# Deformable sampling from 8 by 8 patches as 64-row products on the two halves of the array

## The chip, the cores and the metric

The kernel runs on one core of one Trainium2 chip. The metric is the device time of one execution in microseconds (us). The numbers of a single execution come from the hardware profiler: its span runs from the first to the last instruction, and the execution's own device time stands beside it.

## The reference

Two layers follow one another on 32 images of 128 channels and 32 by 32 pixels. Both start with a group norm and end by adding their input. Layer 0 is an encoder to 1024 channels, a long convolution, a gated linear unit (GLU), a layer norm and a decoder. Layer 1 is the part that the change touches: a deformable depthwise convolution of 8 by 8 taps. Cut to what matters:

```python
x = x + layer0(gn(x))                       # encode, convolve, gelu, GLU, layer norm, decode
off = conv3x3_depthwise(gn(x), offset_w) + offset_b        # (B, 2, 64 taps, H, W)
def body(acc, tap):
    off_t, koff_t, w_t = tap
    px = gx[None] + koff_t[0] + off_t[..., 0]
    py = gy[None] + koff_t[1] + off_t[..., 1]
    ix = px * sx - 0.5;  iy = py * sy - 0.5
    # bilinear sample s of gn(x) at (iy, ix), zero outside the image, for all channels
    return acc + s * w_t[None, :, None, None]
acc, _ = lax.scan(body, zeros, (off, koff, wt))
x = x + gelu((acc - bn_mean) * inv + bn_beta)
```

The offsets are shared by all channels; the tap's weight differs by channel. So a sample is a product of an image patch (pixels by channels) with a column of bilinear weights (pixels by output positions), and the tap's weight is applied to the result.

## The kernel before

**Stages.** First comes a small table (`ssm_kernel_table`), then `ssm_convolution` (the encoder and the long convolution, output `y_d` in DRAM), then `main_block`, then a test that sends images whose offsets are larger than `BOUND_X`, `BOUND_Y` through a general routine (`deformable_redo`).

**main_block** interleaves two streams of work in a written-out order. `first_part(b)` is the GLU, layer norm and decoder of image b: 292 matrix products of 128 rows, 128 columns and 512 moving columns, 584 passes, since each fp32 product is a pair of weight load and matmul twice over. `second_part(b)` is the deformable layer of image b. `run_along` takes the next step of the stream that is behind by its planned cost; `measure` is the planned cost of a step of `second_part`. In the steady state the GLU of image b + 2 runs along `second_part(b)`, and the preparation of image b + 1 (`prepare`, a list of steps with due places) hangs on the same steps. So images 0 to 29 are sampled beside a GLU; images 30 and 31 are sampled alone (`ALONE`).

**Preparation.** The nine 3 by 3 taps give the offsets (`taps`, VectorE). `spread` writes them to DRAM in the order (piece, padded column u, tap column j, tap row, y), `gather` reads them back as 128 partitions, and `hat` makes the one-dimensional bilinear weights on ScalarE: 8 positions in x and 16 in y, 24 tables of `HSUB` = 624 values a partition, written to DRAM (`dhat`). `turn` transposes the image and writes it to DRAM as pixels by channels (`vt_d`).

**Sampling.** The padded columns u = x + kx, 1 to 37, are grouped in 17 packs with a common x window of 8 pixels (`PACKS`); a pack has m = 8 to 16 slots (pairs of column and tap column), 254 in an image. A pack is four pieces of two tap rows (`KY2`). For each piece, `load_hat` loads the x weights (`ds`, SBUF tile of 128 partitions by m by 64) and the y weights (`dhy`, the same size), both replicated to the 16 by 8 pixels of a window by the DMA's access pattern, and `weights` multiplies them on VectorE (L1076). Then three products, one for each of the y windows 0, 8 and 16 (`rows_of`), of 128 rows (16 by 8 pixels), 128 channels and m x 2 x ny columns go to a bank of PSUM each (L1119, tile `dps`, four buffers, tag "sam"); VectorE multiplies each with the tap weights into `prod` (L1122, tile `dp`), and GpSimd adds the two tap rows (L1139) and adds the result into the image's accumulator, column by column (L1144, tile `dacc`). The buffers: five of `ds`, four of `dhy`, three of `prod`.

**Queues.** All loads of hats, windows and `y_d` are issued in the written order by SyncE (queue q1); writes of hats and outputs by ScalarE (q10); the convolution's output `y_d` by GpSimd (q0). Each engine runs its instructions in the written order.

## Time and profile before

| what | value |
|---|---|
| median of 3 runs | 13423.51 us (13420.09 to 13425.37) |
| profiled execution, its own device time | 13421.61 us |
| its span | 13419.9 us, 133500 instructions |
| mean granted TensorE clock | 0.988 |
| TensorE matmul busy | 12998.3 us, 97% of the span |
| VectorE busy | 8388.1 us, 63% |
| ScalarE busy | 3279.7 us, 24% |
| GpSimd busy | 9064.3 us, 68% |
| SyncE's DMA queue (q1) | 2591.60 MB, 72.0% of 16 engines' span |

How to read it: matmuls (PE) and weight loads (PEld) are shown as two rows of one engine, and since matmuls are pipelined, the mean duration of one is longer than the distance between two starts. The distance of starts is what a pass costs in a stream. "x" counts passes, two for each fp32 product. A stage is read in its own window: the convolution takes until 1280 us; then come two GLU images alone; then 30 images of sampling beside a GLU; and from 12880 us two images of sampling alone.

### The profile page before, as it was taken

What the parts mean: (1) busy time and instruction counts of PE and PEld (TensorE: products, weight loads), DVE (VectorE), ACT (ScalarE), POOL (GpSimd) and SP (SyncE); (2) the same over time, 40 slices, a digit from 0 to 9 for tenths busy, and PEclk for the clock granted to TensorE, in tenths of its full rate; (3) what the DMA queues carried; (4) which work ended last, traced back from release to release, by engine and by line L of the source; (5) the groups of instructions that cost most, each with busy time, mean ns of one, the idle gap of its engine ahead of it and who ended that gap; (6) DMA issues with size and microseconds to landing.
All of it is one profiled execution on the core that took longest, in us unless ns stands there. A gap on an engine that the chain in (4) does not pass through costs nothing.

```text
span 13419.9 us, 133500 instructions
## 1 busy us (share of the span) xinstructions
PE 12998.3 (97%) x40482; PEld 7208.8 (54%) x40482; DVE 8388.1 (63%) x12173; ACT 3279.7 (24%) x4767; POOL 9064.3 (68%) x8871
## 2 busy tenths in 40 slices
PE   7998999999999999999999999999999999999975
PEld 7998445555555555555555555555555555555533
DVE  5554146666666666666666666666666666666677
ACT  4433122222222212112222222211122222221245
POOL 2554147777777777777677777777777777777778
PEclk8999999999999999999999999999999999999988
DMA  7998068888888888888888888888888888888866
GB/s 232 274 284 267 19 172 235 240 235 236 232 230 240 236 228 228 233 231 239 237 237 232 229 239 239 231 225 232 231 240 236 236 232 231 236 240 232 232 194 174
DMA packets 1721768, 3055.43 MB, mean 228 GB/s; under 512 B 445523, under 2 KB 1024467, under 8 KB 1720019
## 3 DMA queue, kind: packets, MB, share of 16 engines
q1 hardware_dynamic: 1508434, 2591.60, 72.0%
q10 hardware_dynamic: 163456, 320.92, 6.6%
q0 software_dynamic: 49152, 134.28, 3.3%
q8 instruction: 328, 5.37, 0.2%
q14 instruction: 398, 3.25, 0.1%
HBM read 2580.03 MB, written 466.06 MB: 227 GB/s over the span
## 4 chain that ended last, share of the span: by engine, by line
PE 86%; DMA 7%; DVE 2%; ACT 2%; issue 1%; POOL 1%; SPq 1%; ACTq 0%; DVEq 0%; POOLq 0%
PE gpg L785 24%; PE gpv L808 24%; PE dps L1119 23%; PE psy L320 5%; DMA ds<-dhat 4%; PE gph L824 3%; PE gpo L713 3%; PE psz L237 3%; DMA dhat<-dh 1%; DVE ds L1076 1%; DMA dhy<-dhat 1%; ACT ds L1068 1%; SPq L1057 0%; DMA u<-u_d 0%; DVE dp L1122 0%
## 5 line engine op out<-in xcount | busy, mean ns | idle before, releaser
L1122 DVE TENSOR_TENSOR dp<-dps,k_weight_slots 128x256 f32<-128x256 f32 (+17 forms) x6528 | 3085.4, 483 | 3084.2 <-PE dps L1119 2908.7
L1119 PE MATMUL dps<-ds,dxw 128*128 128x256 f32 (+18 forms) x13056 | 4698.9, 447 | 227.5 <-DVE ds L1076 185.6
L1144 POOL TENSOR_TENSOR dacc<-dacc,dp 128x256 f32<-128x256 f32 (+3 forms) x4736 | 4403.9, 930 | 398.3 <-DVE dp L1139 28.5
L1119 PEld LDWEIGHTS dps<-ds,dxw 128*128 128x128 f32 x13056 | 2468.8, 192 | 3213.9 <-issue 2543.1
L785 PE MATMUL gpg<-gy,g_w_glu 128*128 128x512 f32 x8192 | 3986.4, 593 | 22.9 <-DMA gy<-y_d 18.2
L808 PE MATMUL gpv<-gy,g_w_glu 128*128 128x512 f32 x8192 | 3974.7, 592 | 0.0
L1139 POOL TENSOR_TENSOR dp<-dp 128x448 f32<-128x448 f32 (+2 forms) x2142 | 2671.9, 1247 | 1898.1 <-DVE dp L1122 1895.4
L1076 DVE TENSOR_TENSOR ds<-ds,dhy 128x1024 f32<-128x1024 f32 (+3 forms) x2176 | 3163.4, 1454 | 783.3 <-DMA ds<-dhat 675.5
L785 PEld LDWEIGHTS gpg<-gy,g_w_glu 128*128 128x128 f32 x8192 | 1544.5, 190 | 1237.0 <-issue 968.4
L808 PEld LDWEIGHTS gpv<-gy,g_w_glu 128*128 128x128 f32 x8192 | 1548.9, 189 | 1157.9 <-issue 915.1
L846 POOL TENSOR_TENSOR gs<-gs,gq 128x512 f32<-128x512 f32 x448 | 633.0, 1413 | 1348.2 <-ACT gq L845 1348.2
L845 ACT ACTIVATE gq<-gr 128x512 f32<-128x512 f32 x448 | 282.2, 630 | 4665.5 <-DVE gr L837 4603.9
L357 POOL DMA_DIRECT2D y_d<-yo x1024 | 589.5, 583 | 694.1 <-ACT yo L344 624.6
L792 ACT ACTIVATE gs<-gpg,k_b_glu 128x512 f32<-128x512 f32 x512 | 351.8, 687 | 2494.1 <-PE gpg L785 2378.0
L981 ACT ACTIVATE dh<-dr,k_minus 128x624 f32<-128x624 f32 x768 | 621.7, 809 | 654.7 <-DMA dhat<-dh 574.2
L320 PE MATMUL psy<-toe,z 128*128 128x192 f32 x4096 | 668.0, 326 | 7.4 <-DVE z L242 5.5
L320 PEld LDWEIGHTS psy<-toe,z 128*128 128x128 f32 x4096 | 663.0, 196 | 11.6 <-DVE z L242 6.8
L816 DVE SCALAR_TENSOR_TENSOR gs<-gpv,k_b_glu,gs 128x512 f32<-128x512 f32 x512 | 379.9, 742 | 437.2 <-PE gpv L808 436.8
L982 ACT ACTIVATE dh<-dh,one 128x624 f32<-128x624 f32 x768 | 626.2, 815 | 25.0
L715 POOL TENSOR_TENSOR gs<-gs,gr 128x512 f32<-128x512 f32 x448 | 631.7, 1410 | 0.0
L824 PE MATMUL gph<-gu,k_W_enc 128*128 128x512 f32 x1024 | 525.9, 595 | 30.1 <-DVE gs L816 30.1
L335 DVE TENSOR_TENSOR psy<-psy,t 128x256 f32<-128x256 f32 (+2 forms) x768 | 333.7, 434 | 346.1 <-ACT t L328 329.3
(163 smaller groups left out, 5810.3 us busy)
## 6 DMA issues: line engine op xcount, KB each, us to landing
dhy<-dhat SPq DMA_DIRECT2D x1536, 512.0 KB
ds<-dhat SPq DMA_DIRECT2D x1440, 512.0 KB
dhat<-dh ACTq DMA_DIRECT2D x768, 312.0 KB
y_d<-yo POOLq DMA_DIRECT2D x1024, 128.0 KB, 4.2
gy<-y_d SPq DMA_DIRECT2D x512, 256.0 KB
u<-u_d SPq DMA_DIRECT2D x224, 512.0 KB
dxw<-dvt_d SPq DMA_DIRECT2D x1248, 64.0 KB
dhy<-dhat SPq DMA_DIRECT2D x256, 224.0 KB
```

The costliest lines, as they stand in the source:

```text
L320: nc.tensor.matmul(ps[:, c // 2, c % 2, :], rows[i][:, (g * CG + c0 + c) // 2, c % 2, :], toe[:, c0 + c, :], start=True, stop=True,)
L715: nc.gpsimd.tensor_add(sums[0], sums[0], r)
L785: nc.tensor.matmul(gate, w_glu[:, k, D + m * P : D + m * P + P], ys[k], start=(k == 0), stop=(k == KD - 1),)
L808: nc.tensor.matmul(val, w_glu[:, k, m * P : m * P + P], ys[k], start=(k == 0), stop=(k == KD - 1),)
L824: nc.tensor.matmul(h, w_enc[:, m * P : (m + 1) * P], u, start=True, stop=True)
L846: nc.gpsimd.tensor_add(sums[1], sums[1], sq)
L982: nc.scalar.activation(t, t, AF.Relu, scale=-1.0, bias=const["one"])
L1076: nc.vector.tensor_mul(s[:, :m], s[:, :m], hy[:, :m])
L1119: nc.tensor.matmul(ps, xw[:, j, :], s[:, :m, :, y0 : y0 + ny], start=True, stop=True)
L1122: nc.vector.tensor_mul(prod[:, :m, :, y0 : y0 + ny], ps, w[:, :, :, None].to_broadcast([P, m, KY2, ny]),)
L1139: adder.tensor_add(prod[:, :m, 0], prod[:, :m, 0], prod[:, :m, 1])
L1144: nc.gpsimd.tensor_add(to, to, prod[:, slot : slot + nj, 0])
```

## The change

A sample now comes from a patch of 8 by 8 pixels. Such a product has 64 rows, and two of them lie on the two halves of the array: "side" 0 on partitions 0 to 63 and side 1 on 64 to 127, each with its own weights (`xw[half, w]`), moving columns and PSUM bank. The padded rows v = y + ky, 1 to 37, are dealt to the sides: 1 to 19 to side 0 and 19 to 37 to side 1 (`NV`, `VBASE`); each side has seven y windows of 8 rows at steps of 2 (`NWIN`). The hats are stored in DRAM as (side, position, u, j, ky, 19 rows), 8 positions in x and 8 in y; a tile of them (`ds`, `dhy`) holds one column u, or two in the packs with four columns (`groups_of`), as 128 partitions by up to 9 slots by 152 cells.

A pack is four pieces again (`blocks_of`): piece 0 holds the ends in five small blocks of 2 to 4 rows, and pieces 1 to 3 hold four values of v for all eight tap rows, in two windows each. For each block, window, hat tile and side there is one product. Two pieces make a burst: all products of pieces 0 and 1 are issued together, into four PSUM banks, then the products of the other stream go on, then come the VectorE products with the tap weights (`scale`), one (piece, side) to a step, then the `weights` of a tile of the next pack, in two parts. At the end of a pack GpSimd adds the eight tap rows, which stand in `prod` as rows of 512 values, shifted so that equal y lie under each other, by seven additions, and then adds the total into the accumulator. `prod` is two fixed tiles, cleared once. The buffers: four of `ds` and two of `dhy`, four temporaries for the GLU in place of five; the software descriptor scratch is set to 4096 bytes.

In the preparation, offsets go to DRAM in two steps: `lay` writes them as they are with gaps (`rel_n`), and `spread` copies them from there, DRAM to DRAM, in runs of 19 values, four times an image; `window` copies the image's windows from `vt_d` to `xw_d`, DRAM to DRAM, 16 times an image; there are 16 hat tables of `HSUB` = 741 values in place of 24 of 624. `BOUND_Y` falls from 3.25 to 2.45. The special handling of images 30 and 31 (a loaded quarter of the x weights that ScalarE copies, and one VectorE addition) is gone.

The diff's core:

```diff
+NV = 19
+VBASE = (1, 19)
+CELLS = 8 * NV
+PIECES = 4
+SIDE = NU * 8 * CELLS
+NCOL = 2 * SIDE
...
-BOUND_X, BOUND_Y = 2.45, 3.25
+NWIN = 7
+BOUND_X, BOUND_Y = 2.45, 2.45
...
+def groups_of(us):
+    if len(us) < 3:
+        return tuple((u,) for u in us)
+    return us[:2], us[2:]
+
+def blocks_of(side, piece):
+    if piece == 0:
+        ends = (
+            (0, 2, 1, 6, 1, 0), (2, 2, 3, 4, 1, 0), (4, 2, 5, 2, 1, 0), (2, 3, 2, 1, 2, 2)
+        ) if side == 0 else (
+            (6, 2, 32, 6, 1, 0), (4, 2, 32, 4, 1, 0), (2, 2, 32, 2, 1, 0), (1, 3, 32, 1, 2, 2)
+        )
+        w = 6 * side
+        return [(b, [(w, 0, b[3])]) for b in ends] + [
+            ((4 * side, 4, 19, 1, 1, 0), [(6 - w, 0, 1)])
+        ]
+    v0 = (7, 20)[side] + 4 * (piece - 1)
+    w = 2 * (piece - 1) + side
+    return [((0, 8, v0, 4, 1, 0), [(w, 0, 2), (w + 1, 2, 4)])]
...
-    SB, HB = 5, 4
+    SB, HB = 4, 2
...
+            def lay(a):
+                    nc.sync.dma_start(at(rel_n[b % 2], a * ASTEP + LEAST + 7 * JSTEP,
+                            [[KSTEP, 8], [-JSTEP, 8], [1, L]]), ...)
+            def spread(a, side):
+                    nc.sync.dma_start(
+                        at(rel_d[b % 2], a * NCOL + side * SIDE,
+                            [[NV, 64], [8 * CELLS, NU], [1, NV]]),
+                        at(rel_n[b % 2], a * ASTEP + LEAST - 7 * H + VBASE[side],
+                            [[KSTEP - 1, 64], [H, NU], [1, NV]]))
...
+            def window(side, r):
+                    nc.sync.dma_start(st["xw_d"][side, :, r],
+                        at(st["vt_d"], (12 * side + r) * W * C,
+                            [[C, W], [2 * W * C, NWIN], [1, C]]))
...
             steps = [
...
-                (71, largest), (74, across), (79, down), (81, spread(0)), (82, spread(1)),
-                (89, gather(0)), (90, gather(1)),
-                *((96 + 82 * i // len(hats), step) for i, step in enumerate(hats)),
+                *((54 + i, window(i // 8, i % 8)) for i in range(16)),
+                (68, largest), (70, across), (74, down), (76, lay(0)), (77, lay(1)),
+                *((81 + 3 * i, spread(i // 2, i % 2)) for i in range(4)),
+                (99, gather(0)), (100, gather(1)),
+                *((106 + 72 * i // len(hats), step) for i, step in enumerate(hats)),
...
+        def weights(h, part):
+            m = sum(span_of(u)[1] for u in halves[h][1])
+            cut = slice(0, (m + 1) // 2) if part == 0 else slice((m + 1) // 2, m)
+            nc.vector.tensor_mul(s_of[h][:, cut], s_of[h][:, cut], hy_of[h][:, cut])
+            if part == 1:
+                hy_of.pop(h)
+                load_hat(h + HB, 1)
...
+                for i in range(0, PIECES, 2):
...
+                    for piece in (i, i + 1):
+                        ps = [psam.tile([P, 512], F32, tag="sam", ...) for side in range(2)]
+                        for parts in zip(blocks_of(0, piece), blocks_of(1, piece)):
+                            for part in range(len(parts[0][1])):
+                                for s, count in zip(tiles_s, counts):
+                                    for side in range(2):
+                                        half = slice(64 * side, 64 * side + 64)
...
+                                        nc.tensor.matmul(
+                                            to[side][:, slot : slot + count, :, r0:r1],
+                                            xw[half, w, :], frm, start=True, stop=True)
+                    yield measure(m)
...
+                    for j in range(4):
+                        due(1 + j)
+                        scale(i + j // 2, j % 2)
+                        yield measure(m)
+                    due(5)
+                    if i // 2 < len(ahead):
+                        weights(ahead[i // 2], 0)
+                        yield measure(m) / 2
+                        weights(ahead[i // 2], 1)
+                    yield measure(m) / 2
+                for h in mine:
+                    load_hat(h + SB, 0)
+                for to, frm in ((2, 0), (3, 1), (4, 6), (5, 7), (2, 4), (3, 5), (2, 3)):
+                    nc.gpsimd.tensor_add(row(to), row(to), row(frm))
...
-    nc = _bacc.Bacc("TRN2", target_bir_lowering=False, num_devices=1)
+    nc = _bacc.Bacc("TRN2", target_bir_lowering=False, num_devices=1, dynamic_dma_scratch_size=4096)
```

## The prediction

> **What bounds the kernel now.** I read the page first: engines, slices, the chain of waits.
>
> ```profile
> PE 12998.3 (97%) x40482; PEld 7208.8 (54%) x40482; DVE 8388.1 (63%) x12173; ACT 3279.7 (24%) x4767; POOL 9064.3 (68%) x8871
> PEclk8999999999999999999999999999999999999988
> DMA  7998068888888888888888888888888888888866
> PE gpg L785 24%; PE gpv L808 24%; PE dps L1119 23%; PE psy L320 5%; DMA ds<-dhat 4%; PE gph L824 3%; PE gpo L713 3%; PE psz L237 3%; DMA dhat<-dh 1%; DVE ds L1076 1%; DMA dhy<-dhat 1%; ACT ds L1068 1%; SPq L1057 0%; DMA u<-u_d 0%; DVE dp L1122 0%
> ```
>
> TensorE sets the time, at full clock. Then the windows: nine images of the steady state, and the two images sampled alone.
>
> ```profile
> core 0: us, PE busy (x) PEld busy (x) DVE busy (x) ACT busy (x) POOL busy (x), PEclk, DMA share, GB/s
> 5368.00:8681.00 3313.00, 3294.60 (x9039) 1691.43 (x9039) 2147.76 (x3017) 692.78 (x918) 2391.35 (x2214) 1.00 0.86 234
> 12880.00:13164.00 284.00, 172.54 (x420) 91.36 (x420) 216.93 (x310) 181.13 (x195) 214.27 (x202) 0.79 0.65 189
> 13164.00:13420.00 256.00, 149.00 (x404) 79.89 (x404) 199.22 (x295) 134.12 (x135) 215.14 (x202) 0.85 0.61 175
> ```
>
> An image costs 3313 / 9 = 368.1 us; in it TensorE is idle for 2 us, VectorE busy for 239, GpSimd for 266, the DMA engines for 86%. Only the last two images wait for something else. Third, the groups of those nine images:
>
> ```profile
> L1119 PE MATMUL dps<-ds,dxw 128*128 128x256 f32 (+17 forms) x3674 | 1314.3, 440 | 10.6 <-DVE dp L1122 10.5
> L785 PE MATMUL gpg<-gy,g_w_glu 128*128 128x512 f32 x2304 | 1128.3, 593 | 1.0 <-DVE gs L816 1.0
> L1076 DVE TENSOR_TENSOR ds<-ds,dhy 128x1024 f32<-128x1024 f32 (+3 forms) x612 | 890.1, 1454 | 213.6 <-DMA ds<-dhat 203.8 <-DMA dhy<-dhat 5.7 <-DMA dhat<-dh 3.8
> L1122 DVE TENSOR_TENSOR dp<-dps,k_weight_slots 128x256 f32<-128x256 f32 (+13 forms) x1837 | 870.3, 483 | 906.2 <-PE dps L1119 859.3 <-POOL dacc L1144 29.6 <-POOL dp L1139 7.1
> L1139 POOL TENSOR_TENSOR dp<-dp 128x512 f32<-128x512 f32 (+3 forms) x612 | 762.4, 1246 | 549.8 <-DVE dp L1122 549.0
> L1144 POOL TENSOR_TENSOR dacc<-dacc,dp 128x256 f32<-128x256 f32 (+6 forms) x1332 | 1237.4, 929 | 104.5
> ```
>
> Sampling is 3674 / 9 = 408 passes an image. Last, what a pass costs in a stream, from the chain in order of time (start, us, what): one GLU pass of 512 columns is 1.72 / 4 = 0.43 us, one pass of 128 columns 41.50 / 368 = 0.113 us.
>
> ```profile
> 284.70 41.50 PE psz L237 x368
> 4999.64 1.72 PE gpv L808 x4
> ```
>
> So the GLU's 584 passes take 251 us of the 368 (eight transposes 1 more), and sampling holds TensorE for 116 us an image, 6.8 us a pack. This is what the change must beat.
>
> **TensorE after.** Products of a pack: piece 0 has 5 blocks x 2 hat tiles x 2 sides = 20, pieces 1 to 3 have 2 windows x 2 tiles x 2 sides = 8 each, 44 in all (22 in the pack of one column), 16 x 44 + 22 = 726 an image, 1452 passes with 128 moving columns or fewer (16 to 96 in piece 0, 128 or less in the others). The moving columns of a side are 127 a slot where the full array had 256. But fewer columns do not make a pass cheaper here, since each has a weight load of its own. The trace shows loads as the limit where matmuls are short (sixteen products of one column, at clock 0.50):
>
> ```profile
> L653 PEld LDWEIGHTS g_fold<-k_ln_beta,k_W_dec x16: 286/333/333, 1297.0 to 1300.1; 128*128 128x128 f32 x16
> 1296.00:1304.00 8.00, 6.71 (x31) 6.66 (x32) 1.81 (x9) 0.00 (x0) 0.00 (x0) 0.50 0.63 164
> ```
>
> Fifteen steps in 3.1 us are 0.21 us a load at half clock, 0.105 at full clock: as much as a pass of 128 columns. So a pass is 0.112 us, long or short, and everything hangs on how the two sides overlap, which no row shows: every product before has 128 rows. Bounds: full overlap 1452 x 0.112 / 2 = 81 us an image; none, 163 us. I take 81, since the sides share neither rows, weights, columns nor bank, and keep 163 for the range.
>
> The Trainium skill's "TensorE: Matmul & The Clock Gate" (Part 3: Packing small matmuls) says that matmuls on different row groups run together, with 3.07 times the rate measured for four groups at 512 columns; no run here shows it. By that rate, 1.53 for two groups, the products would take 163 / 1.53 = 106 us and the total be 13540; its case has long matmuls, behind which loads hide.
>
> Entering and leaving the 64-row form: 34 bursts, 68 changes an image. No row prices one. Nothing, if the array takes both forms side by side; at most one matmul's tail and a load: a 128-column pass lasts at least 276 ns where starts are 112 apart, so 0.164, plus a load's 0.19, makes 0.35 us. That is 0 to 24 us an image; I take the tail alone, 11 us, as loads are seen to run under matmuls in flight. The page "TensorEngine Tiling (Array Packing)" (Tiling Modes, Key Properties) speaks against the change: changing the tiling mode drains the array. No run here shows it; by that rule a change costs at least the tail, 11 us an image, and without it nothing.
>
> **VectorE.** From L1122's forms (256 values 415 ns, 480 values 655) an operation is 141 ns + 1.07 a value. Per full pack, 10 small ones of piece 0 (48 to 192 values) and 6 of 512 make 6.6 us, 107 an image (now 97). `weights` goes from 68 operations of mostly 1024 values (512 values 839 ns, 1024 1528: 150 + 1.35 a value) to 66 of mostly 608, some 0.94 us each: 62 us in place of 890.1 / 9 = 99. Sum: 239 + 10 - 37 = 212 us, beside TensorE. But it is coupled more tightly: a burst takes all four banks, so it waits for the previous burst's four scalings, and the first burst of a pack for the weights issued 0.5 step before it. Between bursts TensorE has half a pack of GLU, 7.4 us; VectorE then has 2.8 to 3.9 us of scaling, 2 of weights, about 0.7 of GLU. Where nine `taps` (1.32 us each) or a layer norm's closing (some 7 us) join, it lags by 2 to 3 us a few times an image: 6 us an image in place of 2, range 2 to 20. Behind a waiting burst stand the GLU products, so this goes straight to the end.
>
> **GpSimd.** 68 additions of two tap rows (1.25 us) become 17 x 7 of about 1.2 (144 us), the 148 into `dacc` become 37 (34 us): 178 against 222. Off the path; two `prod` tiles give a pack of slack.
>
> **DMA.** Hats fall from 66.6 MB an image (254 x 256 x 4 B x 128 x 2) to 39.5. New: 4 x 2496 runs of 76 bytes and 3584 of 512, DRAM to DRAM. 128-byte packets take 15 ns of an engine in the trace, 512-byte ones 32: 9 and 7 us of the 16 engines together, far under what the hats free (27 MB, some 110 us of transfer). All go through SyncE's queue, ahead of hat loads; a `window` there also waits for `vt_d` to land. I cost this at nothing: it is covered by tiles loaded a pack ahead, and if that cover fails a stall like today's 10 us at `ds<-dhat` comes a few times an image. The smaller descriptor scratch touches only the convolution's stores: GpSimd waits 42 us for those in all now; nothing. The reference's inputs give offsets of at most 2.38 in x and 2.10 in y, under 2.45, so no image goes to the general routine.
>
> **Sum.** An image: 251 + 1 + 81 + 11 + 6 = 350 us against 368, 18 less; 30 images, 540. The two images alone take 284 and 256 us; their chain runs over loads, VectorE and ScalarE's copy, which is gone. VectorE then needs 169 us, GpSimd 178, products 92: with the coupling I take 230 each, 80 us less in all (0 to 140). From the profiled execution's 13421.6 us (span 13419.9): 13421.6 - 620 = 12800. The median of the runs is 2 us higher, which is nothing beside the rest. A difference of 0.2% (27 us) is about what can be told from no change. This case alone, with 0 to 24 us of changes and 2 to 20 of waits: 12450 to 13300.
>
> **The rivals.**
> *The loads go one at a time* (slower). Place: the weight load in each of 1452 passes. In the trace a load starts when the matmul before it starts, and in the written order both passes of side 0 precede those of side 1, so side 1 may never start early. Price: 163 us in place of 81, an image of 432, 30 x 64 = 1920 more, tail 60 less: 15280. It decides from the point where a pass costs over 0.068 us: (116 - 17) / 1452. For it: the fold's even load spacing, and every stream above. Against: those are loads into the same rows.
> *Half overlap.* Side 1's first pass runs beside side 0's second, but each side's own second load waits: some 0.288 us a pair (two loads 0.21, plus two starts of 34 to 40 ns after a load, the fold's 68 at half clock). 363 x 0.288 = 105 us, image 374, + 180 - 80: 13500, 13250 to 13750.
> *The bound moves to VectorE or the hat loads.* VectorE needs 212 of 350 us and is not it on average; a lag at each burst of 3 us (34 x 3 = 102 us) would undo everything: 30 x (344 + 102 - 368) - 80 more, some 15700. Little speaks for it but the coupling.
>
> **How the numbers follow.** Full overlap 0.47, half 0.21, loads one at a time 0.26, VectorE or transfers 0.06. Faster: nearly all of the first and a quarter of the second, 0.50; same 0.04; slower 0.46. The range must take in part of the loads' case to leave out 0.2: 12450 to 15300.
>
> **What would show it.** Right: 1452 passes an image at `dps`, starts of the two sides within some tens of ns, a burst of pieces 2 and 3 in about 1.8 us; images 350 us apart; PE still busy over 95% in the steady state; DMA share near 0.7; VectorE near 212 us an image. Wrong: passes evenly 0.11 us apart and bursts of 3.6 and 6.3 us (loads), image distance over 368; or idle PE before bursts released by `dp` or `ds` (VectorE). A gap over 0.35 us at the edges of bursts would fail the price of a change.

## The result

The changed kernel takes 14571.98 us, the median of four runs (14553.06 to 14581.83), and the kernel before 13424.44 beside it: a ratio of 1.0851, interval 1.0832 to 1.087. It is 1148 us slower where 624 faster was forecast. The profiled execution has a span of 14577.5 us.

First the page of the changed kernel: busy time, TensorE's clock and the DMA share in 40 slices, and the chain of waits by line.

```profile
PE 13374.9 (92%) x73890; PEld 8152.3 (56%) x73890; DVE 7794.9 (53%) x14251; ACT 2697.3 (19%) x3983; POOL 7930.1 (54%) x6987
...
PEclk9999999999999999999999999999999999999955
DMA  7986277777777777777777777777777777777776
...
PE gpv L837 16%; PE dps L1208 15%; DMA ds<-dhat 14%; PE gpg L814 13%; DVE ds L1132 8%; PE psy L320 5%; DVE prod L1225 3%; PE psz L237 3%; DMA dxw<-dxw_d 3%; PE gpo L742 2%; DMA dhy<-dhat 1%; PE gph L853 1%; SPq L1120 1%; SPq L734 1%; DMA dh
```

TensorE is no longer what sets the time throughout. Its share falls from 97% to 92%, and "DMA ds<-dhat", the x-hat loads, rises from 4% of the chain to 14%, as much as TensorE's products or either half of the GLU. The DMA engines are busy for 70 to 79% in most slices. Then the windows, in the columns of before: eight steady images and the two sampled alone.

```profile
core 0: us, PE busy (x) PEld busy (x) DVE busy (x) ACT busy (x) POOL busy (x), PEclk, DMA share, GB/s
5454.40:8662.80 3208.40, 3017.18 (x16390) 1712.69 (x16386) 1765.09 (x3210) 537.15 (x689) 1834.61 (x1490) 0.94 0.75 159
13872.00:14244.00 372.00, 195.47 (x1558) 178.80 (x1558) 193.82 (x377) 41.48 (x48) 190.84 (x159) 0.56 0.73 156
14244.00:14577.00 333.00, 170.30 (x1365) 158.45 (x1364) 158.25 (x327) 2.30 (x2) 185.16 (x159) 0.57 0.67 129
```

An image costs 3208.40 / 8 = 401 us. TensorE is idle for 24 of them, ten times as long as before, and the clock is 0.94. The DMA engines were busy for 86% at 234 GB/s before; now for 75% at 159, so an engine's busy time brings a fifth less. The two images alone run at little more than half the clock. The groups of those images show each term of the prediction's sum:

```profile
L1254 POOL TENSOR_TENSOR prod<-prod 128x512 f32<-128x512 f32 (+3 forms) x952 | 1265.3, 1358 | 673.4 <-DVE prod L1225 662.8
...
L1208 PE MATMUL dps<-ds,dxw 64*128 64x128 f32 (+6 forms) x11622 | 894.4, 307 | 144.2 <-DVE ds L1132 90.1 <-DMA dxw<-dxw_d 52.2 <-DVE prod L1225 0.4
...
L1225 DVE TENSOR_TENSOR prod<-dps,k_weight_slots 128x512 f32<-128x512 f32 (+14 forms) x2176 | 781.8, 407 | 594.1 <-PE dps L1208 408.6 <-POOL prod L1254 132.0 <-DVE prod L1225 2.3
L1132 DVE TENSOR_TENSOR ds<-ds,dhy 128x608 f32<-128x608 f32 (+2 forms) x530 | 593.5, 1158 | 585.9 <-DMA ds<-dhat 542.2 <-DMA dhy<-dhat 20.2 <-DMA dxw<-dxw_d 12.0
...
L1260 POOL TENSOR_TENSOR dacc<-dacc,prod 128x256 f32<-128x256 f32 (+6 forms) x296 | 198.6, 671 | 23.2
```

VectorE's products now wait for "DMA ds<-dhat" for 542.2 / 8 = 68 us an image, against 203.8 / 9 = 23 before. The engine is not short of time (1765 / 8 = 221 us busy). Its tiles are late.

To separate work from waiting, images are cut where the memset of `dacc` starts, over 20 steady images. Idle time of TensorE and the work that half clock loses (half of the busy time in the stretches with a granted clock of 0.5) are taken off, and what is left is TensorE's work at full clock. In us an image:

| kernel | image | idle | lost to half clock | work | the two images alone |
|---|---|---|---|---|---|
| before | 368.2 | 2.2 | 0.2 | 365.8 | 533 |
| after | 400.5 | 23.4 | 20.3 | 356.8 | 697 |
| e1: y-hats in one load, 16 engines | 387.8 | 16.2 | 14.2 | 357.4 | 575 |
| e2: the same rows in two loads, 8 engines | 397.4 | 22.3 | 18.1 | 357.0 | 678 |
| e3: y-hats issued by GpSimd | 382.3 | 15.7 | 8.9 | 357.7 | 580 |
| e4: before, y-hats in two loads | 437.9 | 51.4 | 15.3 | 371.2 | 654 |
| e5: no copies | 380.5 | 10.5 | 13.4 | 356.7 | 677 |
| e6: e3, spread by GpSimd too | 379.2 | 13.9 | 8.0 | 357.3 | 592 |
| e9: e3 and e5 | 364.5 | 3.8 | 3.1 | 357.6 | 561 |
| e13: e3, spread in 16 parts | 372.2 | 7.8 | 6.9 | 357.5 | 572 |
| e15: e3, no spread | 364.0 | 3.7 | 2.6 | 357.6 | 559 |
| e17: e3, spread in 32 parts | 364.0 | 3.3 | 3.3 | 357.4 | 587 |

The change did make TensorE's work 9 us an image shorter; but idle time and half clock together rose from 2 to 44 us.

### The profile page after: what moved, and what is told of

It reads as the page before. It is cut to its first block, busy times and chain, and to the rows that moved or that the text cites. A ratio compares the mean times of both kernels' runs of the same rounds, so it can differ in the third digit from the quotient of the medians.

```text
span 14577.5 us, 194927 instructions
## 1 busy us (share of the span) xinstructions
PE 13374.9 (92%) x73890; PEld 8152.3 (56%) x73890; DVE 7794.9 (53%) x14251; ACT 2697.3 (19%) x3983; POOL 7930.1 (54%) x6987
## 4 chain that ended last, share of the span: by engine, by line
PE 55%; DMA 22%; DVE 14%; issue 4%; SPq 3%; ACT 1%; POOL 0%; DVEq 0%; ACTq 0%; POOLq 0%
PE gpv L837 16%; PE dps L1208 15%; DMA ds<-dhat 14%; PE gpg L814 13%; DVE ds L1132 8%; PE psy L320 5%; DVE prod L1225 3%; PE psz L237 3%; DMA dxw<-dxw_d 3%; PE gpo L742 2%; DMA dhy<-dhat 1%; PE gph L853 1%; SPq L1120 1%; SPq L734 1%; DMA dhat<-dh 1%
## 5 line engine op out<-in xcount | busy, mean ns | idle before, releaser
L1254 POOL TENSOR_TENSOR prod<-prod 128x512 f32<-128x512 f32 (+3 forms) x3808 | 5057.7, 1357 | 2900.9 <-DVE prod L1225 2858.2
L1208 PE MATMUL dps<-ds,dxw 64*128 64x128 f32 (+14 forms) x46464 | 3700.6, 313 | 842.8 <-DVE ds L1132 384.9
L1225 DVE TENSOR_TENSOR prod<-dps,k_weight_slots 128x512 f32<-128x512 f32 (+16 forms) x8704 | 3128.0, 407 | 2345.8 <-PE dps L1208 1641.5
L1208 PEld LDWEIGHTS dps<-ds,dxw 64*128 64x128 f32 x46464 | 3371.4, 212 | 1722.5 <-issue 959.9
L814 PE MATMUL gpg<-gy,g_w_glu 128*128 128x512 f32 x8192 | 3915.1, 622 | 199.9 <-DMA gy<-y_d 196.7
L837 PE MATMUL gpv<-gy,g_w_glu 128*128 128x512 f32 x8192 | 3832.5, 611 | 0.0
L1132 DVE TENSOR_TENSOR ds<-ds,dhy 128x608 f32<-128x608 f32 (+2 forms) x2112 | 2371.3, 1161 | 2384.4 <-DMA ds<-dhat 2174.6
L1260 POOL TENSOR_TENSOR dacc<-dacc,prod 128x256 f32<-128x256 f32 (+6 forms) x1184 | 797.0, 673 | 92.9
L1022 ACT ACTIVATE dh<-dr,k_minus 128x741 f32<-128x741 f32 x512 | 464.3, 907 | 1143.1 <-DMA dr<-rel_d 776.8
L237 PE MATMUL psz<-w_enc,u 128*128 128x128 f32 x4096 | 495.7, 284 | 18.2 <-issue 10.5
```

The costliest lines, as they stand in the source:

```text
L237: nc.tensor.matmul(both[:, g, j, :], u[:, lo : lo + P], w_enc[:, k * P : (k + 1) * P], start=True, stop=True,)
L814: nc.tensor.matmul(gate, w_glu[:, k, D + m * P : D + m * P + P], ys[k], start=(k == 0), stop=(k == KD - 1),)
L837: nc.tensor.matmul(val, w_glu[:, k, m * P : m * P + P], ys[k], start=(k == 0), stop=(k == KD - 1),)
L1132: nc.vector.tensor_mul(s_of[h][:, cut], s_of[h][:, cut], hy_of[h][:, cut])
L1208: nc.tensor.matmul(to[side][:, slot : slot + count, :, r0:r1], xw[half, w, :], frm, start=True, stop=True,)
L1225: nc.vector.tensor_mul(bass.AP(tensor=at_y.tensor, offset=at_y.offset, ap=[at_y.ap[0], [H, m], [step * (KS - 1) + skew, rows], [1, run],], ...
```

## The experiments

Times are medians; e2, e4, e5, e8, e9 and e15 are one execution each. Two theories stood against each other and against a third. A: the y-hat loads (tile `dhy`) of 64 partitions run on 8 of the 16 DMA engines, so that the x-hats (tile `ds`) that share these engines come late. B: the copies from DRAM to DRAM (`lay`, `spread`, `window`) hold the loads up. The rival C is the prediction's own last one: VectorE, or tiles asked for too late, so that what remains late is late for lack of buffers.

**e1 and e2: sixteen engines or eight.** In the trace of the changed kernel just 8 DMA engines are at work for 19.6% of the steady time (before 1.6%); which ones, the trace does not say. A y-hat load reads with an outermost dimension of 8. e1 makes it one load with 16 outermost, by which the y-hats of a side come in another order and the sums are wrong; e2 keeps this order of rows but two loads:

```
-   for side in range(2): ... at(src, frm + side * 8 * SIDE, [[0, 8], [SIDE, 8], [1, nj * CELLS]])
+e1 at(src, frm, [[SIDE, 16], [0, 8], [1, nj * CELLS]])                              # one load
+e2 for side in range(2): ... at(src, frm + side * 8 * SIDE, [[SIDE, 8], [0, 8], [1, nj * CELLS]])
```

> The changed kernel with each tile of y weights (dhy) loaded by one transfer whose outermost dimension has 16 entries, in place of two whose outermost dimension has 8. The 16 source rows and the bytes are the same, but within a side the rows are laid out in the order of the x weights, so the samples use wrong y weights; all else is as in the change. Theory T1 (the eight-row transfers run on only 8 of the 16 DMA engines, which are then full): no more stretches with exactly 8 active packets (now 20% of the time), VectorE's wait for ds<-dhat falls from 68 us an image to under 15, images 360 to 370 us apart in place of 401, total 13200 to 13450. Rival R1 (the DRAM-to-DRAM copies in SyncE's queue delay the hats) and rival R2 (too few tiles, loads issued too late): image distance stays within 2% of 401, total 14300 to 14600. Rival R3 (the 64-row products or their change of form hold TensorE): total as the change, 14570.

> As the run above it (same source rows and same wrong order of y weights), but again two transfers of 64 partitions whose outermost dimension has 8 entries. It tells the number of engines apart from the order of the rows. T1: as the change, images 395 to 405 us apart, total 14500 to 14700. If the row order were what matters: as the run above.

Measured: e1 14089.93 us, ratio to before 1.0496 (1.0478 to 1.0513); e2 14481.19. The stretches with exactly 8 engines at work fall to 1.2% in e1 and stay at 16.2% in e2. So one load over 16 engines in place of two over 8 is worth 391 us, the order of the rows at most 91. The size of the whole effect was missed: e1 is 664 us over the time before.

**e3: the same loads from another queue.** The two y-hat loads are left as they are, issued by GpSimd.

```
-   nc.sync.dma_start(to[side * 64 : side * 64 + 64], ...)
+   nc.gpsimd.dma_start(to[side * 64 : side * 64 + 64], ...)
```

> The changed kernel with the y weights' transfers issued by GpSimd in place of SyncE, otherwise the same transfers and the same result. T1 if that queue's eight engines rotate from transfer to transfer: no more stretches at exactly 8 active packets, images 365 to 380 us apart, total 13300 to 13800 (74 issues of about 0.6 us more an image on GpSimd, which is at half load). T1 if they are the same eight: as the change, 14500 to 14800. R1: a gain of at most half, since the copies then delay only ds: 14000 to 14500. R2 and R3: as the change.

Measured: 13926.23 us, ratio 1.0366 (1.0349 to 1.0383), 646 us less than the changed kernel. Exactly 8 engines: 3.6% of the time. The wait of VectorE for x-hats falls from 542 to 113 us in a window of eight images. A holds, with an image 18 us shorter, and 15.7 us of idle TensorE remain; the total is 126 us above the range that A had.

**e4: the cut alone, in the kernel before.** Its y-hat load is split into two of 64 partitions; nothing else is touched.

```
-   dims = [[[0, rows], [NCOL, 8]], [[NCOL, rows], [0, 8]]][a]     # one load, 16 outermost
+   for top in range(2): ... at(..., [[NCOL, 8], [0, 8], [1, m * SLOT]])
```

> The kernel before with each load of y weights cut into two transfers of 64 partitions whose outermost dimension has 8 entries; same bytes, same result, 68 issues more an image. T1: the low eight engines must carry 33.3/8 + 33.3/16 MB of hats and 1.1 MB of the rest an image, 7.4 MB, which at 16 GB/s an engine (4096 bytes in 254 ns) takes 460 us: images over 440 us apart, total over 15600. R1, R2, R3: within 1% of 13424, since the copies, the buffers and the products are those of before.

Measured: 15638.62 us, 2212 more than before, with images 437.9 us apart (over 440 was expected) and exactly 8 engines at work for 23.3% of the steady time. From its page, clock, DMA share, rate and the group of `weights`:

```profile
PEclk9999999999999999999999999999999999999987
DMA  7893377777777777777777777777777777777753
GB/s 236 277 283 118 114 195 194 193 202 196 197 196 193 198 203 202 191 203 197 194 193 195 194 200 186 196 207 201 193 196 193 198 196 199 194 195 203 191 169 134
...
L1086 DVE TENSOR_TENSOR ds<-ds,dhy 128x1024 f32<-128x1024 f32 (+3 forms) x2176 | 2834.8, 1303 | 5456.7 <-DMA ds<-dhat 4354.0
```

"ds<-dhat" becomes the longest wait of `weights`, as in the changed kernel, although the x-hat loads were not touched. This shows A by itself, but for one rival: the cut also makes more loads, and each issue takes SyncE some 0.6 us. The traces speak against it. SyncE's issues of loads take 154 us in an image of 368 before, 138 of 400 after the change and 216 of 438 in e4, and for most of the rest it waits. That the cut costs more here than in the changed kernel fits the hats, of which before loads 1.7 times the bytes.

**e5: no copies.** `lay`, `spread` and `window` return at once from the third image on.

> The changed kernel with the DRAM-to-DRAM copies (the image into lay, spread, and window) left out from the third image on, so that later images sample with the places and windows of the first two; everything else is as it was. In the changed kernel's trace TensorE's idle time in eight steady images is 24 us an image, and 14 of it lies in a few places at the eighth and ninth of the 17 packs, just where the four spread copies are issued; SyncE's issues of spread and of the loads behind it take up to 13.6 us there, where before none took over 2.3. Theory (SyncE's queue stands behind spread): the idle time at those packs goes, with some slow clock after it, and images come 13 to 22 us closer, 14570 to some 13870 - 14150, and the issues take 0.3 to 2.5 us. Rival (only the y-hat loads on 8 engines matter): no more than the copies' own DMA time, some 16 us of 16 engines an image of which little is on the path: 14400 to 14570. Rival (no copies on the path, VectorE's coupling is the rest): 14500 to 14570.

Measured: 13996.39 us, 20 us an image less, as B's theory had it. The idle time at the ninth pack, the one of one column, is gone (12.2 us an image from its first product to the next pack's in the changed kernel, 0.0 now); the waits for "ds<-dhat" that A explains are still there, 374 us in 2900.

**e9: both.** e3's and e5's edits together.

> The y-hat loads issued by GpSimd (e3) and the copies lay, spread and window left out from the third image on (e5), both in one kernel. In the changed kernel a steady image of 400.5 us is 356.8 of TensorE's work at full clock, 23.4 of idle TensorE and 20.3 lost to half clock; e3 alone took 18.2 us off an image, e5 alone 20.0, neither changed the 357. Theory (these two are the whole stall): together they take off 36 to 42, an image is 359 to 364 us with under 3 us of idle, and the total 13230 - 13400 with e3's shorter tail. Rival (a third cause, such as VectorE's lag behind the bursts, takes over): an image of 368 to 380, 13550 to 13850.

Measured: 13392.19 us, within the theory's range; an image is 364.5 us, 3.8 of it idle, each a little above what the theory had. Apart, the two edits took 18.2 and 20.0 us off an image; together 36.0. So A and B are all but some 7 us of the stall, and VectorE's coupling (C) has at most these. The two also lie in different places: e3 takes the idle time of the other packs from 11.2 us an image to 3.4 and leaves 12.3 at the ninth, e5 clears the ninth and leaves 10.5 at the others.

**e6, e7, e10: is it the queue, or the number of buffers?** e3's timeline of SyncE's queue, at an eighth pack (start, us, what):

```profile
8127.48 24.14 SPq L990 DMA_DIRECT2D rel_d<-rel_n  x3
8151.72 4.81 SPq L734 DMA_DIRECT2D gy<-y_d  x3
8156.62 6.04 SPq L1115 DMA_DIRECT2D ds<-dhat  x2
8162.71 2.01 SPq L1146 DMA_DIRECT2D dxw<-dxw_d  x2
8164.82 1.08 SPq L734 DMA_DIRECT2D gy<-y_d  x2
...
8172.84 0.54 SPq L1115 DMA_DIRECT2D ds<-dhat  x1
8176.27 2.13 SPq L1146 DMA_DIRECT2D dxw<-dxw_d  x2
```

Three issues of `spread` hold SyncE's queue for 24 us, and inputs of the GLU, x-hats and windows stand behind them. In the same kernel's view of transfers, over 8130 to 8165 us, the DMA engines are at least 80% busy in nine slices in which they bring less than 100 GB/s (slices of 0.9 us, busy tenths and rate):

```profile
DMA  6899899999999998669589989757336999899798
GB/s 117 273 306 263 260 299 220 229 211 255 168 183 186 118 76 36 58 78 97 34 139 247 168 58 25 13 18 49 23 21 41 62 80 61 66 124 115 110 165 207
```

e6 issues `spread` from GpSimd; e7 adds an x-hat tile, e10 a third window tile loaded two packs ahead, both with hat tiles of 8 columns in place of 9 (e7 also with 10 GLU tiles in place of 11).

```
e6  -   nc.sync.dma_start(at(rel_d[b % 2], ...      +   nc.gpsimd.dma_start(at(rel_d[b % 2], ...
e7  -   SB, HB = 4, 2                               +   SB, HB = 5, 2
e10 -   windows(b, n + 1)                           +   windows(b, n + 2)
```

> The changed kernel with the y-hat loads and the four spread copies issued by GpSimd in place of SyncE: the same transfers. With the y-hat loads alone moved (e3) it was 13926 and an image 382.5 us, 15.8 us of it idle TensorE, nearly all of that at the eighth and ninth packs. Theory (SyncE's queue stands behind spread): that idle time and the slow clock after it go, an image comes to 364 - 372 us and the total to 13350 - 13650. Rival (spread's 2496 small pieces load the DMA engines or hold GpSimd's queue as they held SyncE's, so the y-hat loads are late in place of the others): 13800 to 14100.

> As e6, with one more x-hat tile (5 in place of 4), so that the tile needed first in a pack is asked for a pack earlier; room for it comes from tiles of 8 columns in place of 9 (the packs of four columns are paired otherwise) and from 10 GLU input tiles in place of 11. Theory (what remains late in e6 is x-hats): 0 to 10 us an image less than e6, and no wait of VectorE for x-hats. Rival (what remains is the passes' own price and slow clock after the bursts): within 40 us of e6, or slower by up to 100 if the GLU's inputs come late with 10 tiles.

> As e6 (y-hat loads and spread issued by GpSimd), with three window tiles, loaded two packs ahead in place of one; room for the third comes from hat tiles of 8 columns in place of 9, with the packs of four columns paired otherwise. In e6 12.9 of 13.9 us of idle TensorE an image lie at the eighth and ninth packs, and the longest waits there are for the window tile (84.5 us in 2900, longest 11.2): the ninth pack has one column and is half as long, so a load asked for at its start has half the time. Theory (windows late behind the spread pieces): that idle time goes, an image is 364 to 370, the total 13400 to 13600. Rival (the spread pieces make whatever is loaded then late, and y-hats or x-hats wait in its place): 13750 to 13870.

Measured: e6 13861.01 us (ratio 1.0325, 1.0308 to 1.0343), e7 13876.11 (1.033, 1.0306 to 1.0353), e10 13840.89 (1.031, 1.0292 to 1.0327). All three theories fell, and the totals are in the rivals' ranges. In e6 no issue on SyncE takes over 4.6 us while images are sampled, but the idle time stays at the same packs: now the window tile and y-hats are late. First e6 (us in total over 2900, times, longest):

```profile
PE dps L1208 <- DMA dxw<-dxw_d: 84.5, 16, 11.2
DVE ds L1132 <- DMA dhy<-dhat: 74.0, 8, 12.2
```

In e10 the window tile is in time, and y-hats and x-hats are late:

```profile
DVE ds L1132 <- DMA dhy<-dhat: 59.0, 10, 11.8
DVE ds L1132 <- DMA ds<-dhat: 46.6, 10, 13.1
```

In e7 the wait for x-hats is gone, as its theory had it, and y-hats are late for 84 us; its rival's reason, the passes' own price, is not what remains. So it is not SyncE's queue alone and not the number of buffers: what is loaded beside `spread` lands late, from either queue.

**e11, e13, e17: the same copies at other times.** e11 issues the four copies in the ninth and tenth packs. e13 cuts them into 16 parts, 2.5 steps apart; e17 into 32, 1.5 steps apart over four packs, and has the three unread matmuls of e16 (below) besides.

```
e11 +   *((106 + 3 * i, spread(i // 2, i % 2)) for i in range(4)),
e13 +   *((79 + 5 * i // 2, spread(i // 8, i // 4 % 2, i % 4)) for i in range(16)),   # [[NV, 16], [8 * CELLS, NU], [1, NV]]
e17 +   *((79 + 3 * i // 2, spread(i // 16, i // 8 % 2, i // 2 % 4, i % 2)) for i in range(32)),   # half of NU each
```

> As e6, with the four spread copies issued at steps 106 to 115 (the ninth and tenth packs) in place of 81 to 90, and gather and the hats after them moved to 124 to 175. Theory (the spread pieces meet the half-long one-column pack by their place): the idle time falls by half or more, an image is 366 to 373, the total 13450 to 13650. Rival (wherever they are issued, some 14 us of idle and slow clock follow): 13800 to 13900. Should the hats come too late for the next image, over 13900.

> y-hat loads issued by GpSimd (as e3), all copies kept on SyncE's queue, but spread cut into 16 parts of 624 pieces, issued 2.5 steps apart (79 to 116, some 5 us between two) in place of four of 2496 at 81 to 90; gather and hats follow at 102 and 121, and 108 to 173. In e3 four such copies keep the 16 engines 88% busy for some 20 us at 84 GB/s. Theory (a stretch in which spread's pieces hold all 16 engines, so that the loads behind it land late): spaced out it is covered; idle TensorE falls from 15.7 us an image to 4 - 7, an image is 364 to 370, the total 13400 to 13550. Rival (the engine time of the pieces, however spaced, comes out of the hats' time): 13750 to 13930. Rival (SyncE's queue is held per piece): 13700 to 13950.

> e16 with spread in 32 parts of some 312 pieces, 1.5 steps apart from 79 to 126 (four packs), gather at 106 and 130, hats from 112 to 172. e13 (16 parts, 2.5 steps apart) had 7.8 us of idle an image, e15 (none) 3.7; lost to half clock 6.9 and 2.6. Theory (the stretch of held engines): idle 4 to 6 and an image 365 to 369, so 90 to 220 us under e16. Rival (the pieces cost their engine time wherever they are): within 60 us of e16. Rival (more issues in SyncE's queue, 0.6 us each, delay the loads): slower than e16 by up to 150.

Measured: e11 13735.65 us (1.0235, 1.0218 to 1.0252), between its theories, with a quarter of the idle time gone (10.7 us an image, 13.9 in e6) and 7.0 of the rest now at the eleventh and twelfth packs; e13 13655.33 (1.0175, 1.0158 to 1.0192), a total 105 us above its theory's range; e17 13434.29 (1.001, 1.0001 to 1.0019). The window of eight images of e17 (columns as above):

```profile
5180.00:8092.00 2912.00, 2887.25 (x16408) 1628.78 (x16405) 1932.33 (x3209) 538.82 (x689) 2086.10 (x2081) 0.99 0.74 175
```

And what VectorE waited for in it (us in total, times, longest):

```profile
DVE prod L1239 <- PE dps L1216: 627.2, 218, 7.0
...
DVE ds L1140 <- DMA ds<-dhat: 54.2, 13, 7.3
...
DVE ds L1140 <- DMA dhy<-dhat: 3.9, 7, 0.7
```

VectorE now waits for TensorE, as it should, and for hats 58 us where it was 562. The bytes and pieces are those of the changed kernel, and the image is as short as without `spread` (e15). So the pieces' engine time as such costs nothing that shows; their coming in one stretch does.

**e15: which copy.** e3 with `spread` alone left out.

> e3 with spread alone left out from the third image on (lay and window are kept, so later images sample with the places of the first two). e9, with lay, spread and window left out, was 13392 with 3.8 us of idle an image; e3, with all, 13926 with 15.7. Theory (spread is nearly all of the copies' cost): 13400 to 13500, idle at most 5 us an image. Rival (the sixteen window copies, 1.8 MB in pieces of 512 bytes, hold as much): 13600 to 13750.

Measured: 13372.36 us, just under its range, 364.0 us an image: as much as with all copies left out (364.5). `lay` and the `window` copies cost nothing that shows.

**e8 and e12: the price of a pass.** In the changed kernel two passes (one of each side) of pieces 1 to 3 start 139 ns apart, those of piece 0 mostly 112. e8 lets piece 1 read 16 values in one run in place of eight runs of 2, piece 2 write so, piece 3 both; its sums are wrong. e12 does it with the sums kept: VectorE writes the product of the hats into tiles of its own, in the order column, y place, y row.

> As e6, but the passes of 128 columns of pieces 1 to 3 use other places of the tiles (so they compute other sums): piece 1 reads its 16 values of a column in one run in place of eight runs of 2, piece 2 writes its output so, piece 3 both. In the changed kernel starts in these pieces are 139 ns apart, in piece 0 112. Theory (runs of 2 when reading cost the 27 ns): pieces 1 and 3 at 112, piece 2 at 139. Rival (writing): 2 and 3 at 112. Rival (it is the 64 rows by 128 columns, whatever their order): all at 139. Where a third of the passes gets to 112, an image is worth some 7 us less than e6: 13300 to 13450 where e6 is 13500.

> As e6, with the product of the hats written by VectorE into a tile of its own (3 of them; x-hats and y-hats are loaded into two tiles each, a whole pack ahead), cells in the order column, y place, y row, so that a pass of pieces 1 to 3 reads 16 values in one run in place of eight runs of 2; GLU input tiles 10 in place of 11. e8 showed 112 ns in place of 139 for a run of 16. Theory: pieces 1 to 3 at 112 ns, TensorE's work 347 to 350 us an image in place of 357, the total 13500 to 13620; VectorE's weights cost as before. Rival (VectorE pays for writing 32 bytes apart, or piece 0, which now reads places 32 bytes apart, takes back what the others gain): 13750 to 14000.

Measured: e8 13767.16 us. Its passes that read one run are 112 ns apart, those that only write one are 139. So it is reading runs of two values that costs 27 ns, and the work falls to 352.0 us an image (357.3 in e6); the image only from 379.2 to 376.9, as 2 us of idle time come back. e12 has all of pieces 1 to 3 at 112 and the work at 352.3, yet takes 14543.41 (1.084, 1.0822 to 1.0858), far above theory and rival: VectorE's operation, which now writes 32 bytes apart and into a tile of its own, takes 1854 ns (1320 in e6), and for 154 us of 2900 TensorE waits for it. e12 does not tell these two changes apart, nor the loss of two x-hat tiles.

```profile
L1142 DVE TENSOR_TENSOR dw<-ds,dhy 128x608 f32<-128x608 f32 (+1 forms) x479 | 849.7, 1854 | 114.9 <-DMA dhy<-dhat 114.9
```

The gain was given back on the engine that was brought in to pay for it, and half clock comes with the idle time (25.7 us lost an image).

**e14 and e16: the two images alone.** Unread matmuls of 512 columns follow each burst of the last two images of e13, eight in e14 and three in e16.

```
+   if b >= B - 2: hot = pglu.tile(...); for _ in range(8): nc.tensor.matmul(hot, ident, w_glu[:, 0, :T], start=True, stop=True)
```

> e13, and in the last two images, which have no GLU beside them, each burst of products is followed by eight matmuls of 512 columns whose result nobody reads (3.4 us at full clock, in a step of some 8.5 us). In e3 these images take 319 + 261 us, 220 of it with TensorE idle, 478 us at half clock, by which 160 us of work is lost. Theory (the granted clock falls since TensorE is half idle, and TensorE's bursts are on the chain): the clock in these images rises from 0.6 to over 0.85, and they take 40 to 120 us less than in e13. Rival (VectorE, GpSimd and the loads set their pace, not TensorE): within 20 us of e13, or up to 60 slower as the extra matmuls delay bursts.

> e13 with three unread matmuls of 512 columns after each burst of the last two images (e14 had eight, 7.07 us a burst; three are 2.7). In e13 these images take 312 + 260 us, 7.7 to 9.2 a burst, 473 us of it at half clock and 163 us of TensorE's work lost by that. Theory (a slow clock stretches the bursts, and the bursts are on the chain): the clock rises above 0.8, and they take 30 to 110 us less: 13545 to 13625. Rival (weights, scalings and loads set the pace): within 20 us of e13.

Measured: e14 13779.17 us (1.0261, 1.0244 to 1.0278); its clock was full there, but eight matmuls take 7.07 us a burst, twice what I wrote, and TensorE itself became the chain. e16 13621.07 (1.0144, 1.0128 to 1.016), 34 us under e13, at the edge of the theory's range; but in the profiles the loss to half clock in these images falls from 163 to 87 us and their time does not (572 and 584), so those 34 us are not shown to be theirs. The slow clock alone does not set them; what does stays open.

**e18: the rest, without the extras.** e17 without the unread matmuls, and with the first image's copies in four parts, since its steps run before any sampling.

> e17 without the unread matmuls in the last two images, and with spread of the first image (prepared before any sampling) in four copies as in the changed kernel; y-hat loads by GpSimd and 32 spaced parts for all other images. Theory (the 32 parts delay the first image, whose steps run by order and not by time): sampling starts 30 to 60 us earlier than e17's 1896, an image stays at 364, the last two at 570 to 590 together, the total 13370 to 13410, 0.1 to 0.4% under before. Rival (the start is set by the queue of y-hat loads on GpSimd): 13425 to 13445.

Measured: 13433.49 us, ratio 1.0009 (1.0 to 1.0018), 23 us above the theory's range. Sampling starts 43 us earlier than in e17, as expected, but an image is 365.6, and the last two take 577. No version that keeps the copies beats the kernel before (e9 and e15, which leave copies out, are 32 and 53 us under it): steady images are 2.6 us (e18) to 4.2 us (e17) shorter, and the first and the last two give it back.

## Why the prediction was wrong

**Overlap of the two sides: right.** It was the largest doubt, with 0.47 against 0.47 for the two rivals on it. A burst of pieces 2 and 3, 32 passes between two of the GLU (start, us, what):

```profile
8009.66 2.48 PE L1208 MATMUL dps<-ds,dxw 64*128 64x128 f32 x32
8012.07 0.70 PE L814 MATMUL gpg<-gy,g_w_glu 128*128 128x512 f32 x1
```

One after the other at 0.112 us they would take 3.6 us; they start within 2.2 us, the passes of the two sides some 5 to 20 ns apart. "Loads one at a time" and "half overlap" are both refuted. Half overlap's 0.288 us for a product of both sides, four passes, is close to what pieces 2 and 3 take, 2 x 0.139 = 0.278, but that is chance: side 1 does not start a pass late, and where a column is read in one run the four take 0.224. Nor does the time, between the two rivals' 13500 and 15280, owe anything to their mechanisms. The Trainium skill's "TensorE: Matmul & The Clock Gate" (Part 3: Packing small matmuls) gives packing less than the full factor (3.07 for four). Here, with a weight load for each pass, e8's passes that read one run show two in the 112 ns of one, the full factor.

**The price of a pass: mis-sized.** 0.112 us was taken for every two passes side by side; 396 such pairs an image (16 packs x 24, and 12 in the pack of one column) take 0.139 where they have 128 columns. That is up to 396 x 0.027 = 10.7 us. Taking the price away gave back half: 5.3 us of work in e8 and 5.0 in e12, where the burst of pieces 2 and 3 falls from 2.18 us between its first and last start to 1.99 and 1.78, but that of pieces 0 and 1 does not (3.31 in e6, 3.32 and 3.39); why is not tested. The row it came from had 128 columns in one run.

**Changes of form: right.** From the last GLU pass to the first product it is 523 ns where passes are 429 apart (94 more), the first pair takes 100 more, the step from the last product to the GLU 90, and the first GLU pass 104: 0.39 us in and out, 34 x 0.39 = 13 us an image where 11 were taken. The page "TensorEngine Tiling (Array Packing)" (Tiling Modes, Key Properties) has a drain at a change of mode; the 0.19 us at either edge agree with it, and the bound of nothing is refuted.

So TensorE's work was put at 251 + 1 + 81 + 11 = 344 us and is 356.8: the two corrections are up to 10.7 and 2.

**Waits: the coupling right, its place not.** 6 us (2 to 20) were taken for the coupling to VectorE. Where the loads are out of the way (e9, e15, e17) idle time and lost clock are 6.3 to 6.9 us. In the changed kernel they are 43.7. VectorE is busy for 221 us an image (212 said; scalings 98 for 107, `weights` 74 for 62), GpSimd's additions take (1265.3 + 198.6) / 8 = 183 (178 said).

**DMA: the step that failed.** "I cost this at nothing: it is covered by tiles loaded a pack ahead." Bytes and engine time were about right: the 76-byte pieces take 10.9 us of the 16 engines an image, 9 were said. Two things were not in the sum. First, a load of 64 partitions was counted as 1/16 of its bytes on each engine. With 8 of outermost dimension it puts twice that on 8 engines, and the x-hats, which use all 16, are late too (e1 to e4). The page "DMA: Bandwidth & Descriptors" of the Trainium skill says it (Why a DMA increments its semaphore by 16 and not by 1, and Rules for kernel authors): the outermost dimension of both sides sets the number of engines. The runs agree with it. It stood in the diff, `[[0, 8], [SIDE, 8], ...]`, and the sum passed over it. Second, 10.9 us were read as a share of 368, when three of the four copies come in one stretch of some 24, and at the one pack that is half as long as the others. There "a pack ahead" is 13 us (e5 and e17; 22 in most others). A stall "like today's 10 us", a few times an image, was named as the price if the cover fails, and left out of the sum. It is 36 us an image (the changed kernel against e9): 19.6 of idle time and 17.2 lost to half clock, for which the sum had no term, less 0.8 by which the work is longer in e9.

**The images alone: wrong.** 460 us for the two were forecast, 697 measured, 559 to 592 with e3's loads. The sum had each engine's own time and took the largest plus something for the coupling; before, the same images showed TensorE busy for 60% and no engine over 80%, which points to a chain, and such a sum can't give that. Of the miss, the loads' part is the 117 us between the changed kernel and e3.

**The sum.** 30 x (400.5 - 350) = 1515 us, of which 30 x 12.8 is TensorE's work and 30 x 37.7 the stall; 697 - 460 = 237 at the end. Together 1752 of the 1772 missed. The range held the time, 12450 to 15300, for the sake of a rival that was not the cause. The case nearest to what happened, hat loads as the bound, had a chance of 0.06 and a price from another mechanism.

## What to carry to other kernels

Read each DMA of a diff by its outermost dimension before its bytes: two loads with 8 outermost in place of one with 16 cost 2200 us in a kernel that was otherwise untouched. Price a transfer by the stretch it comes in and by what is due in that stretch, not by its share of the whole, and look for the shortest step of the loop, where the cover is thinnest; spreading the same pieces over time gave back what leaving them out did. And an idle TensorE can be paid twice: with 23 us of gaps an image came 20 us lost to half clock.

## What was not expected of the hardware

- With loads issued by GpSimd some VectorE operations are longer; why is not tested. The taps take 2085 ns in e3, 1309 in the changed kernel, one addition on `drel` 6690 in place of 1743; in e1, where SyncE issues all loads, 1271 and 1432. The products of the hats take 1281 in place of 1158, but 1263 in e1 too, so that is not the queue. The first two groups in the changed kernel, 5300 to 8200 us:

```profile
L946 DVE SCALAR_TENSOR_TENSOR dco<-dv,k_offset_w,dco 128x961 f32<-128x961 f32 (+1 forms) x56 | 73.3, 1309 | 0.0
...
L974 DVE TENSOR_TENSOR drel<-drel,k_base_y 128x1024 f32<-128x1024 f32 x7 | 12.2, 1743 | 0.0
```

And in e3, in the same stretch:

```profile
L946 DVE SCALAR_TENSOR_TENSOR dco<-dv,k_offset_w,dco 128x961 f32<-128x961 f32 (+1 forms) x64 | 133.4, 2085 | 0.0
...
L974 DVE TENSOR_TENSOR drel<-drel,k_base_y 128x1024 f32<-128x1024 f32 x8 | 53.5, 6690 | 0.0
```

- The same y-hat loads leave exactly 8 engines at work for 19.6% of the time from SyncE's queue and 3.6% from GpSimd's. That fits eight engines that stay the same from load to load on the first queue and change on the second, which the trace does not show directly.
- Moving values read in runs of two 4-byte values cost 139 ns for 128 columns on each side, one run 112.
- A load issued beside copies of 2496 pieces of 76 bytes lands late: SyncE's issues there took up to 13.6 us in the changed kernel (before at most 2.3 while images were sampled), and in e3 the engines are at least 80% busy at 61 to 80 GB/s in four slices in a row.
